# Putting out half of the channels during the last pass of attention: a two-layer convolution and attention kernel on one core

## The chip, the core and the metric

The kernel runs on one core of a Trainium2 chip. The metric is device time in microseconds, from the start of the program on that core to its end. Times below that carry a position, such as "at 3327.8", are counted from the start of the profiled span.

## What is computed

Two layers work on `x`, 2 images of 512 channels and 64 x 64 pixels in float32. The first is a deformable convolution with a residual; the change doesn't touch it. The second is attention within each image, a product with `Wfc`, a batch norm and a ReLU, and again a residual. Cut to its core:

```python
q = tanh(px @ Wq.T); k = tanh(px @ Wk.T); v = px @ Wv.T
attn = softmax(einsum('bip,bjp,p->bij', q, k, align_w))
content = (px + attn @ v) @ Wfc.T + bfc
c = transpose(content, (0, 2, 1))                  # images, 512 channels, pixels
mean, var = over images and pixels, per channel
x = x + relu(gamma * (c - mean) / sqrt(var + eps) + beta)
```

Mean and variance of a channel are over both images and all pixels. So no value of a channel can be put out before the last pixel of the last image has its content in that channel. Channels don't depend on each other.

## The kernel before

**Layout.** The 512 channels lie as 4 blocks of 128 partitions. The kernel calls blocks 0 and 1 the lower half (h = 0) and blocks 2 and 3 the upper half (h = 1). The 4096 pixels of an image are 8 columns of 512 (`qb`). A piece is one half by one column, [128, 2, 512] in float32, 0.524 MB; the result is 2 images x 8 columns x 2 halves = 32 pieces. The second layer's input, the residual of the last step, lies in DRAM as `x1_d`; the content before the norm goes to DRAM as `c_d`.

**Attention.** Images are taken in order, n = 0 and 1. In each, four chunks of two columns of queries are worked through; a chunk is 63 slots (7 products over 9 groups of keys), and a slot keeps TensorE busy for about 3 us (`slot`, with `products` at line 1501). After every ninth slot `collect` (1524) takes the sum out of PSUM; it is a generator that is resumed slot by slot. In the 54th slot the last product that the lower half needs ends; `finish` (1509) scales by the softmax's totals, adds the bias, and takes batch norm statistics into `bst` (1522) for that half, by slot 57. The product that ends with slot 62, the last, completes the upper half. The content of the last chunk (image 1, columns 6 and 7) isn't written to DRAM but stays on chip, in `kept`.

**Tiles.** A ring of 38 tiles of a piece's size (`piece`, 1252) feeds the whole stage: keys' exponentials, contents, residuals. In the last chunk of the last image it is less and less used. From slot 22 on, one call of `fetch` (1264) per slot lends free tiles to the final stage: it loads the residual `xr` (1267) and, where it isn't kept, the content `cr` (1271) of the next piece in the list `waiting`. The rule for it is `live + len(taken) + 2 <= 36`, where `live` counts the tiles that attention still needs. Three further tiles, two of the keys' and one of the queries', are lent first (`spare`). These loads are issued by POOL (`nc.gpsimd`), and each waits there until its ring tile is free. SP (`nc.sync`) issues the attention's own loads of `v` (1487) in the meantime, three slots ahead. Behind the last slot come `at.rest()`, which finishes the last `collect`, loads by SP for the rest of the ring (up to 34 taken), and for 8 fresh tiles (`fin`, 1810).

**The final stage.** One batch norm of all four blocks (1815 to 1822) gives scale and shift. Then for each piece, in the order image 1 before image 0, column by column, both halves of a column in turn: two ReLU activations with scale and shift on ACT (1829), one add of the residual on DVE (1832), one store on POOL (1833). The tile of the residual is then free for the next load, the tile that is stored after three further pieces; refills are issued by SP. The program ends with a test whether the fast path was allowed (551 to 570): a small identity matrix (`ident_f`) made on POOL, a transpose on TensorE, three steps on DVE, a register load on every engine, and a branch around the general path, whose code is long.

Engines issue their own instructions in program order and wait on semaphores. In this stage the order is written by hand (`manual_schedule`), so the order of calls in the source is the order in each engine's queue, except for the closing test, which stands outside of it.

Of the kernel before, what the change touches and what calls it, by code (L numbers as in the profile page):

```python
# [10 lines left out]
F32 = mybir.dt.float32  # L11
I32 = mybir.dt.int32
AF = mybir.ActivationFunctionType
# [5 lines left out]
P = 128  # L19
NB = 2  # L20
# [554 lines left out]
def window_path(ctx: ExitStack, tc: tile.TileContext, t_in: dict, out: bass.AP, far: bass.AP, sums: bass.AP):  # L575
# [67 lines left out]
    with ExitStack() as l0:  # L643
# [298 lines left out]
        def fetch(i, s):  # L942

            if i >= NSEQ:
                return
            n, ch = divmod(i, NCH)
            t = io.tile([P, PX, C], F32, name="patch", bufs=2)
            for p in range(PX):
                nc.sync.dma_start(
                    t[:SN, p, :], xt_d[n][ch * ROWS + PR * s : ch * ROWS + PR * s + SY, PC * p : PC * p + SX, :]  # L950
                )
            patches[i, s] = t
# [289 lines left out]
    with ExitStack() as l1, tc.manual_schedule():  # L1242
# [15 lines left out]
            taken.append(name)  # L1258
            return piece(name)

        waiting = deque((n, qb, h) for n in reversed(range(NB)) for qb in range(NCH) for h in range(2))
        ready = deque()

        def fetch(new, queue):
            n, qb, h = waiting.popleft()
# [8 lines left out]
        with ExitStack() as inner:  # L1274
# [33 lines left out]
            def sum_pixels(engine, pair):  # L1308

                (a_lo, a_hi), (b_lo, b_hi) = pair  # L1310
                s = [piece("xs") for _ in range(4)]
                engine.tensor_add(s[0], b_lo, b_hi)
                engine.tensor_sub(s[1], s[0], a_lo)
                engine.tensor_sub(s[2], a_lo, b_lo)
                engine.tensor_sub(s[3], a_hi, s[1])
                return s
# [53 lines left out]
            def query_tile():  # L1370
                return lent.tile([P, 2, CH], F32, tag="q", name="q")
# [348 lines left out]
            for n in range(NB):  # L1720
                at = Attention(n)
                first = at.chunks[0]

                for i in range(NCH // 2):
                    if 0 < i < 3 or n and i == 0:
                        k = i + 1 if i else 1
                        pixels[k] = load_pixels(n, k, nc.gpsimd)
                    pk = pair_bank("pk")
                    for h in range(2):
                        for kb in range(KB):  # L1730
                            nc.tensor.matmul(
                                pk[:, h, :], wkq[:, kb, h : h + 2].rearrange("p h d -> p (h d)"),
                                pixels[i][h][kb // 2][:, kb % 2, :], start=(kb == 0), stop=(kb == KB - 1),
                            )
                    qt = piece("qt", (P, CH))
                    for h in range(2):
                        rk, rq = slice(h * DQ, (h + 1) * DQ), slice((1 - h) * DQ, (2 - h) * DQ)
                        nc.scalar.activation(qt[rq], pk[rq, h, :], AF.Tanh)
                        nc.scalar.activation(keys[rk, i, :], pk[rk, h, :], AF.Tanh)
                    nc.scalar.activation(qt, qt, AF.Identity, scale=al)  # L1740
                    for h in range(2):
                        nc.scalar.dma_start(q_d[n][i][:, h, :], qt[(1 - h) * DQ : (2 - h) * DQ, :])
                    if i == 0:
                        first.q = load_queries(n, 0)
                    if i:
                        psums[i] = sum_pixels(nc.vector, pixels[i])
                    for t in range(4):
                        if t % 2 == 0:
                            raw = []
                        raw.append(piece("vform", (P, 2, 4, P)))  # L1750

                        def between(stage):
                            event = EARLY.get((i, t))
                            if event and stage == 2:
                                for done in at.open:
                                    settle(*done)
                                produce(first, *event)
                                at.open = [(first, *event)]
                            step(2)

                        values(t, pixels[i], psums[i], wc, wcs, raw[-1], between)
                        if t in (1, 2) and i + 1 < NCH // 2:
                            for h in range(2):
                                normalize(pixels[i + 1][t - 1][h], 2 * h, *norms[n])
                        if t % 2:
                            g = 2 * i + t // 2
                            fill.append(filling(*raw, v_d[n][g], piece if g + 1 == NG else None))
                        if i == 3 and t == 2:
                            for s in range(3):
                                at.fetch(s)  # L1770
                    pixels.pop(i)
                    psums.pop(i)
                for s in range(LEAD):
                    at.sums(s)
                for s in range(NCH // 2 * SLOTS):
                    if s == 0:
                        at.at(-7, first, s)
                    if s == 2:
                        at.at(-3, first, s)
                    at.slot(s)  # L1780
                    if s < 5:
                        step(2)
                    if n == 0 and s in (92, 94, 96, 98, 101, 103):
                        next(later, None)
                    l = s - (NCH // 2 - 1) * SLOTS
                    if n + 1 < NB:
                        if l == 47:
                            pixels[0] = load_pixels(n + 1, 0, nc.gpsimd)
                        if l == 49:
                            wc = value_output()  # L1790
                        if l == 51:
                            wcs = sum_value_output(wc)
                        if l in (52, 53):
                            for h in range(2):
                                normalize(pixels[0][l - 52][h], 2 * h, *norms[n + 1])
                        if l == 55:
                            psums[0] = sum_pixels(nc.vector, pixels[0])
                    elif l >= 22:
                        if l == 22:
                            room = key_tile()  # L1800
                            spare = deque((room[:, 0:2], room[:, 2:4], query_tile()))
                        live = 6 + sum(last + g >= l for last in (18, 41, 45, 54) for g in range(NG + 1))
                        if len(spare) > 1 or live + len(taken) + 2 <= 36:
                            fetch(lambda name: spare.popleft() if spare else ring_piece(name), nc.gpsimd)
                at.rest()
                if n + 1 == NB:
                    while len(taken) + 2 <= 34:
                        fetch(ring_piece, nc.sync)

        fin = l1.enter_context(tc.tile_pool(name="w1fin", bufs=8, reuse_waits="tile"))  # L1810
        for _ in range(4):
            fetch(lambda name: fin.tile([P, 2, CH], F32, tag="f", name=name), nc.sync)
        bmv = bnp.tile([P, KB, 2], F32, name="bmv")
        for kb in range(KB):
            nc.vector.bn_aggr(bmv[:, kb, :], bst[:, kb, :, :].rearrange("p a b -> p (a b)"))
        bsc = bnp.tile([P, KB], F32, name="bsc")
        nc.scalar.activation(bsc, bmv[:, :, 1], AF.Sqrt, bias=eps)
        nc.vector.reciprocal(bsc, bsc)
        nc.vector.tensor_mul(bsc, bsc, gamma)
        bsh = bnp.tile([P, KB], F32, name="bsh")  # L1820
        nc.vector.tensor_mul(bsh, bmv[:, :, 0], bsc)
        nc.vector.tensor_sub(bsh, beta, bsh)
        free, stored = deque(), deque()
        while ready:
            n, qb, h, ct, xr = ready.popleft()
            ct = kept.pop((qb, h)) if ct is None else ct
            for r in range(2):
                k = 2 * h + r
                nc.scalar.activation(
                    ct[:, r, :], ct[:, r, :], AF.Relu, bias=bsh[:, k : k + 1], scale=bsc[:, k : k + 1]  # L1830
                )
            nc.vector.tensor_add(ct, ct, xr)
            nc.gpsimd.dma_start(out_v[n, :, 2 * h : 2 * h + 2, qb * CH : (qb + 1) * CH], ct)  # L1833
            free.append(xr)
            stored.append(ct)
            if len(stored) > 3:
                free.append(stored.popleft())
            while waiting and len(free) > 1:
                fetch(lambda name: free.popleft(), nc.sync)


# [45 lines left out]
```

## Time and profile before

| what | value |
|---|---|
| median of 3 runs | 3409.13 us |
| lowest, highest | 3407.39, 3413.03 us |
| the profiled execution's own time | 3413.08 us |
| its span | 3411.3 us |
| PE busy | 3152.2 us (92%) |
| DVE busy | 2755.0 us (81%) |
| ACT busy | 1349.5 us (40%) |
| POOL busy | 435.7 us (13%) |
| last product of attention ends at | 3327.8 us |
| first store of a result is issued at | 3340.58 us |
| last store is issued at | 3398.05 us |

The profile is of one execution. Its page gives busy time by engine, the span in 40 equal slices, the DMA queues, the chain of work that ended last, and the costliest groups of instructions. Its trace can be asked for any stretch of the span: which instruction ran when, what it waited for, and how many bytes DMA moved. PE is TensorE, DVE VectorE, ACT ScalarE, POOL GpSimd; SP only issues DMAs. A name such as `out<-cr` means that `out` is written from tiles that the program calls `cr`. A tile keeps the name of its first use: a refill can be `cr<-wx`, a residual loaded into a tile once named `cr`; `wx` is `x1_d` and `wc` is `c_d`.

### The profile page before, as it was taken

The numbers are of one execution on the slowest core, as the hardware profiler recorded it, in microseconds if no ns is written. First come the engines' busy times: TensorE is split into PE (matmuls) and PEld (weight loads), VectorE is DVE, ScalarE is ACT, GpSimd is POOL, SyncE is SP. The second block draws the span as 40 slices with busy tenths as digits, with TensorE's granted clock in tenths as the row PEclk, the third lists the DMA queues.
The fourth block names the chain that finished last, engine by engine and source line by source line (L and its number), as shares of the span: only waits on it lengthen the run. The fifth ranks groups of instructions, "written<-read, shape, count | busy, mean of one in ns | idle before, by whom it ended". The sixth has DMA issues, their size and how long they took to land. (4 is left out here: it accounts for less than half of the span.)

```text
span 3411.3 us, 38291 instructions
## 1 busy us (share of the span) xinstructions
PE 3152.2 (92%) x14147; PEld 2265.2 (66%) x14147; DVE 2755.0 (81%) x3826; ACT 1349.5 (40%) x1802; POOL 435.7 (13%) x474
## 2 busy tenths in 40 slices
PE   5789999999999899899999999999899999999990
PEld 2355555555555567687787877887587787787880
DVE  8899999998999568786885976968697696885975
ACT  2477788788877533202213112023211202203105
POOL 2112111211121001001001010000101101001112
PEclk9799999999999999999999999999999999999995
DMA  6333443344333268758658667657866758658788
GB/s 227 104 99 116 136 125 111 93 127 128 101 97 117 98 233 268 235 181 236 190 167 222 197 192 207 202 189 247 256 196 193 208 185 236 185 170 223 240 296 356
DMA packets 238388, 629.98 MB, mean 185 GB/s; under 512 B 28112, under 2 KB 45136, under 8 KB 237168
## 3 DMA queue, kind: packets, MB, share of 16 engines
q1 hardware_dynamic: 181456, 431.07, 37.8%
q0 software_dynamic: 43936, 159.40, 18.0%
q10 hardware_dynamic: 12800, 36.97, 3.0%
q8 instruction: 114, 1.87, 0.2%
q14 instruction: 82, 0.67, 0.1%
HBM read 410.15 MB, written 124.91 MB: 157 GB/s over the span
## 5 line engine op out<-in xcount | busy, mean ns | idle before, releaser
L1501 PE MATMUL accy<-tt,v 128*128 128x256 f32 x2016 | 601.3, 380 | 0.8 <-DVE ct L1530 0.6
L1413 ACT ACTIVATE e<-pS 128x1024 f32<-128x1024 f32 x256 | 248.3, 1021 | 727.2 <-PE pS L1408 723.0
L1501 PE MATMUL accx<-e,v 128*128 128x256 f32 x1792 | 471.6, 386 | 0.0
L1501 PE MATMUL accy<-e,v 128*128 128x256 f32 x1792 | 461.3, 380 | 0.0
L820 DVE SCALAR_TENSOR_TENSOR conv<-xn,L_conv_dw_w_sb,conv 128x504 f32<-128x504 f32 (+1 forms) x512 | 409.4, 808 | 37.5 <-ACT conv L814 23.6
L1501 PEld LDWEIGHTS accy<-tt,v 128*128 128x128 f32 x2016 | 384.3, 191 | 53.8 <-DVE ct L1530 1.0
L1501 PEld LDWEIGHTS accx<-e,v 128*128 128x128 f32 x1792 | 334.2, 191 | 120.8 <-issue 80.6
L1501 PEld LDWEIGHTS accy<-e,v 128*128 128x128 f32 x1792 | 342.2, 191 | 46.1
L1480 DVE TENSOR_TENSOR tt<-e 128x256 f32<-128x256 f32 x448 | 187.7, 419 | 178.5 <-PE accy L1501 149.6
L1481 DVE TENSOR_TENSOR tt<-tt,e 128x512 f32<-128x512 f32 x448 | 310.0, 692 | 15.3
L1501 PE MATMUL accx<-tt,v 128*128 128x256 f32 x1008 | 301.3, 381 | 5.1 <-DVE tt L1480 5.1
L984 PEld LDWEIGHTS pa<-bt,patch 96*128 96x128 f32 x2048 | 249.6, 196 | 57.5 <-issue 34.9
L1408 PE MATMUL pS<-q,keys 64*128 64x512 f32 x1024 | 257.9, 623 | 15.3 <-ACT e L1413 15.3
L984 PE MATMUL pa<-bt,patch 96*128 96x128 f32 x2048 | 253.5, 281 | 7.7 <-ACT bt L970 6.3
L970 ACT COPY bt<-pb 96x1024 f32<-96x1024 f32 x124 | 235.1, 2009 | 58.1 <-PE pb L965 58.1
L789 PE MATMUL pq<-in_w,xn 128*128 128x512 f32 x512 | 240.5, 614 | 6.8 <-DVE o L882 4.6
L1004 PE MATMUL py<-dT,L_conv_out_w_sb 128*128 128x512 f32 x512 | 236.6, 607 | 4.8 <-ACT dT L995 4.8
L1506 ACT COPY u<-accx 128x256 f32<-128x256 f32 x56 | 20.8, 372 | 519.7 <-PE accx L1501 517.0
L1501 PEld LDWEIGHTS accx<-tt,v 128*128 128x128 f32 x1008 | 192.2, 191 | 32.0 <-DVE tt L1480 6.3
L877 PE MATMUL po<-om_w_pg,feat 128*128 128x432 f32 x512 | 204.8, 546 | 2.3 <-ACT feat L860 2.3
L995 ACT COPY dT<-pa 32x256 f32<-32x256 f32 x496 | 179.6, 362 | 66.0 <-PE pa L984 56.7
L1422 POOL DMA_DIRECT2D tot<-e x144 | 124.0, 887 | 583.5 <-DVE e L1398 277.7
(242 smaller groups left out, 4331.4 us busy)
## 6 DMA issues: line engine op xcount, KB each, us to landing
v<-wv SPq DMA_DIRECT2D x436, 448.0 KB
tot<-e POOLq DMA_DIRECT2D x176, 512.0 KB, 7.0
patch<-xt SPq DMA_DIRECT2D x256, 192.0 KB
v<-ww SPq DMA_DIRECT2D x56, 448.0 KB
wv<-vform SPq DMA_DIRECT2D x48, 512.0 KB
wv<-vsum SPq DMA_DIRECT2D x48, 384.0 KB
xt<-xj SPq DMA_DIRECT2D x128, 128.0 KB
res<-in_x SPq DMA_DIRECT2D x64, 256.0 KB
```

The lines of the kernel that those rows point to most:

```text
L789: nc.tensor.matmul(pq, xn[:, kb, 1 + 2 * t : 3 + 2 * t, :].rearrange("p r c -> p (r c)"), in_w[:, kb, :], start=(kb == 0), stop=(kb == KB ...
L820: nc.vector.scalar_tensor_tensor(dst, src, wt, dst, ALU.mult, ALU.add)
L877: nc.tensor.matmul(po[:, : 3 * GP], f[:, kb, t * P : (t + 1) * P], om_w[:, kb].rearrange("p a k g -> p (a k g)"), start=(kb == 0), stop=(k ...
L970: copy(bt[:SN].rearrange("s g q d -> s d (g q)")[:, d0 : d0 + 4, :], pb[:SN])
L984: nc.tensor.matmul(pa[:, p], xp[:SN, p, cb * P : (cb + 1) * P], bt[:SN, 4 * cb : 4 * cb + 4, PX * s + p, :], start=True, stop=True,)
L995: copy(dst, src)
L1004: nc.tensor.matmul(py, out_w[:, kb, cb * P : (cb + 1) * P], dT[:, kb, :], start=(kb == 0), stop=(kb == KB - 1))
L1408: nc.tensor.matmul(p[:, a, :], keys[r, i, (2 * u + h) * P : (2 * u + h + 1) * P], c.q[r, qh, :], start=True, stop=True,)
L1413: nc.scalar.activation(e.rearrange("p a q -> p (a q)"), p.rearrange("p a q -> p (a q)"), AF.Exp)
L1480: nc.vector.tensor_sub(t[:, 0], x[:, 1], x[:, 3])
L1481: nc.vector.tensor_add(t[:, 1:3], t[:, 0].unsqueeze(1).to_broadcast([P, 2, HQ]), x[:, 0:3:2])
L1501: nc.tensor.matmul(out, v[:, blk, :], op, start=(first and g == 0), stop=(final and g == NG))
```

## The change

The list of pieces is put in another order: all lower halves (image 1, then image 0), then all upper halves. The batch norm is split in two, of two blocks each (`batch_norm(h)`). The lower one runs behind slot 57 of the last chunk. In slots 58 to 62 one piece each is put out (`put_out`: two ReLUs, an add, a store), and from slot 60 free tiles are refilled at once (`refill`). In turn nothing is fetched ahead in slots 57 to 62. One more tile is lent ahead: `early`, which held the weights of keys and queries and isn't used any longer. Behind the last slot the rest of the ring is filled (SP), then the last `collect` is resumed step by step with a piece put out between the steps, then comes a refill, and the upper norm, with a further piece between its halves. The loop over the remaining pieces is as before.

```diff
-        waiting = deque((n, qb, h) for n in reversed(range(NB)) for qb in range(NCH) for h in range(2))
-        ready = deque()
+        waiting = deque((n, qb, h) for h in range(2) for n in reversed(range(NB)) for qb in range(NCH))
+        ready, free, stored = deque(), deque(), deque()
+        scales = {}
+
+        def batch_norm(h):
+
+            mv = bnp.tile([P, 2, 2], F32, name=f"bmv{h}")
+            for r in range(2):
+                nc.vector.bn_aggr(mv[:, r, :], bst[:, 2 * h + r, :, :].rearrange("p a b -> p (a b)"))
+            sc, sh = bnp.tile([P, 2], F32, name=f"bsc{h}"), bnp.tile([P, 2], F32, name=f"bsh{h}")
+            nc.scalar.activation(sc, mv[:, :, 1], AF.Sqrt, bias=eps)
+            yield
+            nc.vector.reciprocal(sc, sc)
+            nc.vector.tensor_mul(sc, sc, gamma[:, 2 * h : 2 * h + 2])
+            nc.vector.tensor_mul(sh, mv[:, :, 0], sc)
+            nc.vector.tensor_sub(sh, beta[:, 2 * h : 2 * h + 2], sh)
+            scales[h] = sc, sh
+
+        def put_out():
+            n, qb, h, ct, xr = ready.popleft()
+            ct = kept.pop((qb, h)) if ct is None else ct
+            sc, sh = scales[h]
+            for r in range(2):
+                nc.scalar.activation(
+                    ct[:, r, :], ct[:, r, :], AF.Relu, bias=sh[:, r : r + 1], scale=sc[:, r : r + 1]
+                )
+            nc.vector.tensor_add(ct, ct, xr)
+            nc.gpsimd.dma_start(out_v[n, :, 2 * h : 2 * h + 2, qb * CH : (qb + 1) * CH], ct)
+            free.append(xr)
+            stored.append(ct)
+            if len(stored) > 3:
+                free.append(stored.popleft())
+
+        def refill():
+            while waiting and len(free) > 1:
+                fetch(lambda name: free.popleft(), nc.sync)
...
+                    elif l > 57:
+                        put_out()
+                        if l > 59:
+                            refill()
+                    elif l == 57:
+                        for _ in batch_norm(0):
+                            pass
                     elif l >= 22:
                         if l == 22:
                             room = key_tile()
-                            spare = deque((room[:, 0:2], room[:, 2:4], query_tile()))
+                            spare = deque((room[:, 0:2], room[:, 2:4], query_tile(), early))
                         live = 6 + sum(last + g >= l for last in (18, 41, 45, 54) for g in range(NG + 1))
                         if len(spare) > 1 or live + len(taken) + 2 <= 36:
                             fetch(lambda name: spare.popleft() if spare else ring_piece(name), nc.gpsimd)
-                at.rest()
                 if n + 1 == NB:
                     while len(taken) + 2 <= 34:
                         fetch(ring_piece, nc.sync)
+                    for _ in at.ends.pop():
+                        put_out()
+                    refill()
+                    norm = batch_norm(1)
+                    next(norm)
+                    put_out()
+                    next(norm, None)
+                at.rest()
...
-        for kb in range(KB):
-            nc.vector.bn_aggr(bmv[:, kb, :], bst[:, kb, :, :].rearrange("p a b -> p (a b)"))
...
         while ready:
...
+            put_out()
+            refill()
```

## What was predicted before the run

> **What bounds the kernel now.** I read the busy shares first, then the table of stretches at the end of the run, then the chain of waits, then single instructions. Over the whole span TensorE is busy 92%, but the change touches only the last 120 us, so that stretch is read alone. Columns: stretch, length, busy time of PE, its weight loads, DVE, ACT, POOL with counts, granted clock, DMA share, GB/s.
>
> ```profile
> 3292.00:3304.00 12.00, 12.00 (x57) 10.60 (x56) 6.81 (x12) 0.37 (x1) 2.11 (x4) 1.00 1.02 410
> 3304.00:3316.00 12.00, 12.00 (x58) 10.58 (x57) 10.83 (x16) 2.56 (x4) 1.58 (x3) 1.00 0.98 351
> 3316.00:3320.00 4.00, 4.00 (x20) 3.54 (x19) 0.00 (x0) 0.00 (x0) 0.00 (x0) 1.00 0.62 230
> 3320.00:3328.00 8.00, 7.76 (x36) 6.49 (x35) 0.89 (x2) 0.37 (x1) 0.00 (x0) 1.00 0.48 171
> 3328.00:3336.00 8.00, 0.18 (x2) 0.11 (x2) 7.08 (x11) 2.62 (x3) 0.00 (x0) 0.66 0.48 159
> 3336.00:3344.00 8.00, 0.37 (x1) 0.08 (x1) 6.06 (x17) 6.79 (x11) 2.58 (x5) 0.50 0.98 349
> 3344.00:3404.00 60.00, 0.00 (x0) 0.00 (x0) 34.82 (x29) 38.96 (x55) 21.15 (x30) 0.50 1.03 418
> 3404.00:3408.00 4.00, 0.00 (x0) 0.00 (x0) 0.00 (x0) 0.00 (x0) 0.00 (x0) 0.50 0.52 212
> ```
>
> Three things: TensorE sets the pace until 3327.8; DMA moves 418 GB/s, its ceiling here, from 3344 to 3406; and between them is a hole, 3316 to 3344, where DMA is half idle. The hole is worth (188·4 + 247·8 + 259·8 + 69·8)/418 = 12.8 us of full DMA. But DMA is also full, or nearly, from 3292 to 3316, with loads ahead for the final stage. The chain of waits over the last 107 us agrees that DMA is the tail:
>
> ```profile
> 3352.10 17.19 DMA out<-cr
> ...
> 3369.84 18.84 DMA out<-cr
> ```
>
> Loads (hardware queue, SP) and stores (software queue, POOL) share it about evenly while both have work (3352 to 3388; packets, MB, share):
>
> ```profile
> q0 software_dynamic: 2156, 7.84, 53.3%
> q1 hardware_dynamic: 1997, 7.25, 49.2%
> ```
>
> The program's very end, from the instructions of line 570, the closing test's branch and what follows it (engine, operation, duration in ns, first and last start):
>
> ```profile
> L570 POOLq EVENT_SEMAPHORE  x5: 17/43/43, 3405.2 to 3406.7; - x5
> L570 PEldq COMPARE_BRANCH  x1: 6455/6455/6455, 3339.2 to 3339.2; - x1
> ...
> L570 POOLq COMPARE_BRANCH  x1: 45/45/45, 3399.2 to 3399.2; - x1
> L570 POOLq INC_SWDGE_SEM  x1: 622/622/622, 3408.0 to 3408.0; - x1
> ```
>
> Each engine jumps over the untaken general path. POOL's jump lasts 3399.2 to 3405.2, 6.0 us (PE's 6.5), hidden: the last store, issued at 3398.05, lands at 3408.0. From there to the end of the span are 3.3 us.
>
> **What the Trainium skill says.** "DMA: Bandwidth & Descriptors", queues, rings and completion order: each DMA engine takes turns between queues with work, a packet at a time. The 7.84 against 7.25 MB agree. The same page, where 436 GB/s comes from: the fabric's ceiling is 435 GB/s; the trace holds 418, so no schedule can make the tail's bytes cheaper. "Runtime: NRT & Kernel Launch", instruction fetch mechanics: a branch to a page not in the window waits for a DMA that fetches it. The jumps of 6.0 and 6.5 us agree, and both were taken beside full DMA.
>
> **The change, part by part.** A tile is 0.524 MB, 1.25 us at 418 GB/s. The final stage has 60 tile loads (32 residuals, 28 contents, four being kept on chip) and 32 stores; the change alters none of these counts, so only idle DMA can be won or lost.
>
> *Loads ahead given up.* Before, one fetch per slot is allowed from slot 22 to 62: POOL issues 32 tile loads, the last seven at 3294.4 to 3312.5, and SP four more at 3318.3 to 3327.4. After, fetches stop at slot 56, because 57 is the norm and 58 to 62 put out. Counting with the kernel's own rule for live tiles, they are 14 fetches, 26 tiles: 4 lent plus 22 of the ring. Ring tiles come free when products end, and the 22nd did so at 3291.4. So POOL loads nothing from there until its first store. Seven tiles, 3.67 MB, leave the 10.05 MB that moved from 3292 to 3320; one lent tile moves ahead of 3292. This is a loss of about 7·1.25 - 1.25 = 7.5 us of DMA work not done ahead.
>
> *First half put out early.* The statistics of slot 57 end at 3313.9. Two aggregates (0.54 each, half of the four at 3334.2) end at 3315.0; from aggregate to first Relu took 1.40 (3336.10 to 3337.50), so 3316.4. The 1.28 us table load lies on an idle ACT. Two Relus 1.52, one add 1.23, 0.31 to the issue: first store 3319.5, the next three 1.41 apart, to 3323.7. The fifth stands behind the last copy of `accx` on ACT (3326.12 + 0.37), so 3329.5. TensorE pays nothing: ACT and DVE are idle from 3316 to 3326, DVE's sums for slot 62 slip by some 2.5 us to 3317.5 and are due at 3324.7, and the last attention load is issued at 3315.7, ahead of any store. If that cover failed, it could cost these 2.5 us. The copy on ACT stands behind puts 1 to 4, but their loads were issued by 3220, so they wait for nothing.
>
> *SP's queue.* Six refills stand ahead of the eleven ring loads. Four follow the first four adds (3319.3 to 3323.5), the fifth waits for the first store to land, the sixth for the fifth add (3329.3); only then come the ring's eleven, free or not. The first nine transfers give 11.3 us of work from 3320.5, to about 3331.8, so the queue stays fed.
>
> *Between the last products.* Three puts are woven into the last collect: 3 adds of 1.23 and 2 Relus of 0.8 delay the upper norm by about 6 us, its Relus are first needed by the 17th put, and DMA has the eleven loads meanwhile. Cost nothing; 6 us if DMA were empty there.
>
> *Sum.* From 3320.5 on, 34 loads and 32 stores remain: 66·0.524 = 34.6 MB, 82.8 us. The first 8 us of such a start ran at 349 (3336 to 3344): +1.3. So 3404.6 with no gap. Now loads (34) do not finish well ahead of stores as before (last load at 3388.3), but last, so the last put is load, Relus, add, issue in a row: 1.52 + 1.23 + 0.31 and about 1.5 until data flow, against some two stores still queued (2.5): a gap of 2.0. DMA ends at 3406.6, the last store lands at 3408.6: +0.6 against 3408.0. Bounds: -3 (no ramp, no gap) to +4 (loads get the smaller share).
>
> *The closing test.* In the built program its two POOL instructions on `ident_f` moved from ahead of the 32 stores to behind them, and TensorE, DVE and all branches wait for them. The last store is issued some 4.2 us ahead of landing (the least shown for `cr`), 3404.4. Then POOL's issue 0.73, the two instructions 0.57, transpose 0.45, three DVE steps 0.67, register load 0.5 to 1.1 (0.9 taken): 3407.7. Then the jump. Beside full DMA it was 6.0; here DMA is all but empty, which no row of before shows. Lower end 1 us, upper 6.5; I take 3.5, since its 16 KB (six packets, 0.05 MB for three engines in the last 24 us) wait for nothing. 3411.2 against landing 3408.6; plus 3.3: the span ends at 3414.5 against 3411.3, +3.2. The profiled execution took 3413.08, 3.95 above the median 3409.13; I carry the difference over to the median: 3412.3.
>
> **The rivals.** *Hole filled for nothing (faster).* If what is lost from 3292 to 3320 were not work done ahead, the hole's 12.8 minus ramp 1.3, gap 2.0 and test 2.6 leaves -6.9; with the test hidden, -9.5: 3400. For it: the hole is plain. Against it: DMA at 351 to 410 GB/s ahead of it is loads of the final stage. *The test's jump in full (slower).* The test stands behind the last store and its jump takes 6.5 as on PE, while loads, with 48% of the shared DMA, end about a microsecond later: 3.2 + 3.0 + 1 = +7.2, 3416.3. It decides from a jump of 0.9 us on (3408.6 - 3407.7), where the landing no longer hides it; for it, the jumps that the trace shows take over 5 us. *Not what it says*: the built order shows the puts ahead of the last products, so no more than a remainder.
>
> **Chances.** A measurement of this kernel tells 0.2%, 6.8 us, from no change. Forecast (3412.3, within 0.2%): 0.64. Filled hole, 3400: 0.12, nearly all of it faster by over 0.2%. Full jump, 3416: 0.24, its centre at the bound, its upper part and some of the forecast's tail slower by over 0.2%. So faster 0.11, same 0.66, slower 0.23. Range 3403 to 3418: the lower end lies between forecast and filled hole, the upper takes in the bounds +4 of DMA and the full jump, short of both at their worst.
>
> **What would show it.** DMA near 150 GB/s between 3300 and 3319, then full from 3321 without a hole to about 3404: right. First store near 3319.5, fifth near 3329.5. Last load landing within 8 us of the last store's issue. The test's register loads after the last store, on all engines together, and POOL's jump ending after the last landing. I am wrong if DMA stays full from 3300 to 3319, if it has a new hole near 3325 to 3345, or if TensorE ends later than 3327.8.

## The result and the profile after

| | before | after |
|---|---|---|
| median, 22 runs each | 3407.17 us | 3412.29 us |
| lowest, highest | 3401.20, 3413.03 us | 3408.44, 3416.08 us |
| ratio, 95% interval | | 1.0015 [1.0009, 1.0021] |
| span of the profiled execution | 3411.3 us | 3409.4 us |
| last product of attention ends at | 3327.75 us | 3320.16 us |
| from there to the end of the span | 83.55 us | 89.24 us |

The change costs 5.1 us, 0.15%: less than the 0.2% bound that the prediction set for "no change", and resolved from zero. Forecast were 3.2 us. The interval of the ratio is 3.1 to 7.2 us, so the forecast lies at its lower end.

The two profiled spans can't be subtracted. The execution of after reached the end of the products 7.6 us earlier, for reasons ahead of the change (a load of `xq` that POOL issues some 240 us ahead of the products' end starts at 3078.5 there and at 3086.1 in before, already 7.6 apart), so I compare **tails**: the time from the end of the last product to the end of the span, 83.55 against 89.24 us, +5.7. One tail of one execution is good to perhaps 2 us. In five profiles whose final stage has the same code (after and, below, e1, e5, e10 and e11; e5 only adds small steps to it) the last store is issued 78.7, 76.4, 77.2, 76.3 and 75.6 us behind the products' end: after's is the latest.

The stretches of after, with the same columns as in the prediction. The same place in before lies 7.6 us later.

```profile
3292.00:3304.00 12.00, 12.00 (x57) 10.58 (x56) 11.03 (x17) 2.19 (x4) 0.00 (x0) 1.00 0.55 169
3304.00:3316.00 12.00, 12.00 (x57) 10.55 (x57) 9.86 (x16) 7.70 (x11) 2.45 (x4) 1.00 0.61 192
3316.00:3320.00 4.00, 4.00 (x20) 3.32 (x18) 0.00 (x0) 1.47 (x3) 0.47 (x1) 1.00 1.01 402
3320.00:3328.00 8.00, 0.35 (x3) 0.11 (x2) 7.48 (x9) 3.13 (x5) 1.61 (x3) 0.83 1.01 385
3328.00:3336.00 8.00, 0.00 (x0) 0.00 (x0) 4.03 (x6) 3.81 (x7) 1.30 (x2) 0.50 1.02 399
3336.00:3344.00 8.00, 0.00 (x0) 0.00 (x0) 6.82 (x10) 8.00 (x12) 3.07 (x5) 0.50 1.03 419
```

The hole behind the products is gone: 385 to 419 GB/s where before had 159 to 349. In its place DMA runs at 169 and 192 GB/s during the last slots. Counted back from the products' end, in steps of 4 us from -28 to -8, before moved 400, 380, 333, 338 and 234 GB/s there, and after 221, 122, 165, 172 and 119. The hole has moved ahead of the products' end. TensorE is busy for the whole of each stretch up to 3320.

The stores that were to begin early, from the instructions of the tile `out` and the timeline (start, duration, engine, line):

```profile
3311.51 0.73 POOL L1288 DMA_DIRECT2D out<-keys  x1 [27.21 <-DVE keys L1287]
3321.87 0.73 POOL L1288 DMA_DIRECT2D out<-cr  x1 [5.39 <-DVE cr L1287]
```

These are the first store, 8.65 us ahead of the products' end, and the fifth, 1.71 behind it. The end of the run, from the timeline:

```profile
3394.84 1.52 ACT L1284 ACTIVATE cr<-cr,bsh,bsc 128x512 f32<-128x512 f32 x2 [3.46 <-DMA cr<-wc]
3396.39 1.23 DVE L1287 TENSOR_TENSOR cr<-cr,xr 128x1024 f32<-128x1024 f32 x1 [3.76 <-ACT cr L1284]
3398.89 0.73 POOL L1288 DMA_DIRECT2D out<-cr  x1 [5.23 <-issue]
3399.62 0.22 POOL masks.py:197 MEMSET ident_f<- 128x128 f32 x1
```

Read the gaps between these rows. The Relus behind the last load start at 3394.84, the add ends at 3397.62, yet the store is issued only at 3398.89: 1.27 us later instead of the 0.3 of the pieces just ahead of it, and the row names nothing that it waited for ("issue"). In the meantime DMA runs dry (GB/s in the last column):

```profile
3388.00:3392.00 4.00, 0.00 (x0) 0.00 (x0) 0.59 (x1) 1.52 (x2) 0.65 (x1) 0.50 1.02 418
3392.00:3396.00 4.00, 0.00 (x0) 0.00 (x0) 0.63 (x1) 1.16 (x2) 0.73 (x1) 0.50 0.97 391
3396.00:3400.00 4.00, 0.00 (x0) 0.00 (x0) 1.23 (x1) 0.36 (x1) 1.03 (x3) 0.50 0.04 17
3400.00:3404.00 4.00, 0.37 (x1) 0.08 (x1) 0.56 (x3) 0.00 (x0) 0.21 (x1) 0.50 0.36 143
```

That last store lands 3.1 us after its issue, at 3402.0. The end of the program comes 7.4 us later. The instructions of the closing test's branch:

```profile
L570 POOLq EVENT_SEMAPHORE  x5: 17/43/43, 3405.9 to 3406.2; - x5
...
L570 POOLq COMPARE_BRANCH  x1: 45/45/45, 3401.9 to 3401.9; - x1
L570 PEldq COMPARE_BRANCH  x1: 3558/3558/3558, 3401.9 to 3401.9; - x1
...
L570 POOLq INC_SWDGE_SEM  x1: 566/566/566, 3406.3 to 3406.3; - x1
```

All engines branch together at 3401.9, behind the register loads. POOL goes on at 3405.9, 4.0 us later and 3.9 us behind the landing; before, POOL's jump was over 2.8 us ahead of the landing. Another 3.5 us end the span (POOL's last steps, called the exit below).

### The profile page after: what moved, and what is told of

Its sections match the earlier page's. It is cut to its first block, busy times and chain, and to the rows that moved or that the text cites. A ratio compares the mean times of both kernels' runs of the same rounds, so it can differ in the third digit from the quotient of the medians.

```text
span 3409.4 us, 38281 instructions
## 1 busy us (share of the span) xinstructions
PE 3147.5 (92%) x14147; PEld 2260.3 (66%) x14147; DVE 2755.4 (81%) x3830; ACT 1350.9 (40%) x1803; POOL 432.7 (13%) x468
## 4 chain that ended last, share of the span: by engine, by line
PE 69%; DVE 19%; DMA 6%; issue 3%; ACT 2%; POOL 1%; SPq 0%; ACTq 0%; POOLq 0%; DVEq 0%
PE accy L1535 21%; PE accx L1535 17%; DVE conv L820 10%; PE pS L1442 6%; PE py L1004 6%; PE pq L789 5%; PE pa L984 5%; PE pvy L1693 3%; PE pvx L1693 2%; PE pk L1765 1%; DVE e L1464 1%; DMA early<-in_x 1%; DMA tot<-e 1%; DMA wv<-vform 1%; DMA wv<-vsum 1%
## 5 line engine op out<-in xcount | busy, mean ns | idle before, releaser
L1535 PEld LDWEIGHTS accx<-e,v 128*128 128x128 f32 x1792 | 333.5, 190 | 121.0 <-issue 80.2
```

What stands on the lines that cost most here:

```text
L1535: nc.tensor.matmul(out, v[:, blk, :], op, start=(first and g == 0), stop=(final and g == NG))
```

## The experiments

Theory: the DMA part of the change nets to about nothing (loads ahead given up, hole filled), and the closing test, now behind the last store, costs what its chain and jump exceed the landing. Rivals: the test is hidden and DMA costs the 5 us; or the loads given up cost their full price.

The experiments were timed in 9 to 21 runs beside 41 to 53 runs of the kernel before (medians 3408.30, 3408.51 and 3408.70 us in the three groups). "Last store" is its issue, counted from the products' end; "steps" are the two longest parts of the exit: the last semaphore step (INC_SWDGE_SEM in the trace) and the longest DRAIN that POOL takes before the program ends, in us.

| run | us | ratio, 95% interval | last store | tail | steps |
|---|---|---|---|---|---|
| before | | | 70.3 | 83.55 | 0.62 + 1.82 |
| after | 3412.29 | 1.0015 [1.0009, 1.0021] | 78.7 | 89.24 | 0.57 + 1.58 |
| e1 | 3408.50 | 1.0003 [0.9995, 1.0011] | 76.4 | 81.01 | |
| e2 | 3407.56 | 0.9998 [0.9989, 1.0006] | 69.7 | 81.00 | |
| e3 | 3405.70 | 0.9996 [0.9987, 1.0004] | 64.9 | 80.81 | 1.33 + 4.76 |
| e4 | 3407.68 | 1.0003 [0.9994, 1.0011] | 74.5 | 84.91 | 0.56 + 1.58 |
| e5 | 3408.74 | 1.0000 [0.9992, 1.0008] | 77.2 | 84.27 | 0.56 + 1.58 |
| e6 | 3403.62 | 0.9987 [0.9981, 0.9994] | 64.0 | 79.98 | 1.33 + 4.76 |
| e7 | 3406.94 | 0.9994 [0.9986, 1.0003] | 63.9 | 82.02 | 1.33 + 4.76 |
| e8 | 3413.47 | 1.0013 [1.0004, 1.0021] | 70.9 | 87.85 | 1.32 + 4.72 |
| e9 | 3407.22 | 0.9993 [0.9986, 1.0000] | 63.6 | 80.70 | 1.32 + 4.73 |
| e10 | 3416.68 | 1.0028 [1.0018, 1.0038] | 76.3 | 90.63 | 1.33 + 4.77 |
| e11 | 3411.73 | 1.0010 [1.0004, 1.0017] | 75.6 | 86.12 | 0.58 + 1.66 |
| e12 | 3413.66 | 1.0012 [1.0003, 1.0020] | 71.5 | 87.83 | 1.31 + 4.69 |

### e1 and e2: both kernels without the closing test

Both leave out lines 551 to 570 of before (and the same lines of after) and the general path behind them; the fast path is whole.

```diff
     window_path(tc, t_in, out, far, sums)
-    with tc.tile_pool(name="flag", bufs=1) as fp, ...
-    ...
-    with tc.If(again > 0):
-    ...
```

> The changed kernel without the closing test and without the general path behind it (that part of the program is left out; the output comes from the fast path alone, as always with these inputs). Theory: behind the last store's issue the changed kernel runs memset, select, transpose, three DVE steps, a register load and a jump in a row, and only then leaves, 3.3 us after the store could have landed (3405.9 against 3398.9 + 3.7). Without them the end follows the landing: about 3.3 us less than the changed kernel, so +1.8 us on the kernel before (ratio 1.0005). Rival, the whole loss is in DMA and the test is hidden as it was before: no gain, +5.1 us (1.0015).

> The kernel before without the closing test and the general path (left out in the same way). There POOL's jump ended at 3405.2 and the last store landed at 3408.0, so theory and rival both expect next to nothing: -1.0 to 0 us (0.9997 to 1.0). If it gains as much as the changed kernel does without its test, the test's place was not what cost there.

Without the test the changed kernel is 0.9 us slower by the medians, 0.05% by the ratios, with intervals that include no difference; the tails are equal, 81.0 and 81.0. From the last store's issue to the span's end after goes from 10.51 to 4.63 us, before from 13.25 to 11.31: the test costs 5.9 us there and 1.9 here, 3.9 more, as much as the jump in after outlasts the landing. In before it isn't quite free even though its jump is hidden, since the landing at 3408.0 is followed by 3.3 us of steps that e2 has only in part. The rival that the test is hidden in after (1.0015) is not seen.

### e3: loads ahead kept going

Fetches go on in slots 57 to 62, beside the norm and the puts. So that POOL, which waits for free tiles, doesn't hold up stores, SP issues the five early ones.

```diff
-        def put_out():
+        def put_out(queue=nc.gpsimd):
...
-                    elif l > 57:
-                        put_out()
-                        if l > 59:
-                            refill()
-                    elif l == 57:
-                        for _ in batch_norm(0):
-                            pass
                     elif l >= 22:
+                        if l == 57:
+                            for _ in batch_norm(0):
+                                pass
+                        if l > 57:
+                            put_out(nc.sync)
+                        if l == 61:
+                            refill()
...
-                    while len(taken) + 2 <= 34:
+                    while len(taken) + 2 <= 33:
```

> The changed kernel with the loads ahead given back: fetches go on by the same rule in slots 57 to 62 on POOL, the five stores of slots 58 to 62 are issued by SP, refills wait for slot 61, and the last ring fill stops one tile earlier. Theory: the DMA work not done ahead from 3292 to 3316 is what the change loses; six tiles more are loaded ahead, 6 x 1.25 = 7.5 us less behind it, of which a hole of up to 3 us near the end of the products may eat some: -7.5 to -4.5 us on the changed kernel, so -2.4 to +0.6 on the one before (ratio 0.9993 to 1.0002). DMA from 3292 to 3312 at over 300 GB/s, counted with this run's own end of the products. Rival, loads ahead are not the loss (they only ran beside attention's loads): +5 us (1.0015).

The stretches of e3, the same columns:

```profile
3292.00:3300.00 8.00, 8.00 (x38) 7.04 (x38) 6.88 (x10) 0.19 (x1) 1.59 (x3) 1.00 1.03 418
3300.00:3308.00 8.00, 8.00 (x38) 7.04 (x38) 7.75 (x13) 3.99 (x6) 0.53 (x1) 1.00 0.98 343
3308.00:3316.00 8.00, 8.00 (x38) 7.03 (x37) 6.58 (x10) 5.89 (x9) 0.00 (x0) 1.00 0.44 118
3316.00:3320.00 4.00, 4.00 (x20) 3.51 (x19) 0.00 (x0) 0.94 (x2) 0.00 (x0) 1.00 1.05 404
3320.00:3328.00 8.00, 0.88 (x6) 0.38 (x4) 6.95 (x9) 3.67 (x6) 0.73 (x1) 0.75 1.03 369
3328.00:3388.00 60.00, 0.37 (x1) 0.08 (x1) 35.31 (x43) 37.41 (x53) 19.41 (x28) 0.50 1.03 419
```

Now both are had: DMA full with loads ahead until 3308 and full again from 3316, with a hole of 118 GB/s between. Its last store lands 72.4 us behind the products' end; in after, at 81.8, and at 79.5 and 79.4 in e1 and e10, whose code is the same up to there. So the DMA work ends 7 to 9 us earlier; six tiles' loads are 7.5 us. Not separated is what the five stores on SP instead of POOL do in it: they were not run without the loads. The time falls by 6.6 us: the program's own end, with test and exit, now stands 8.4 us behind the last landing instead of 7.4. The test is less of it (POOL's jump ends 1.0 us behind the landing instead of 3.9), and the exit, of which the last experiments speak, is more.

### e4: three stores held back for the gap

In the last loop the stores of three pieces that are ready early are issued just ahead of the last piece, to have DMA work while that piece is loaded, normed and added.

```diff
...
+        keep = []
         while ready:
-            put_out()
+            if len(ready) == 1 and not waiting:
+                for to, ct in keep:
+                    nc.gpsimd.dma_start(to, ct)
+            put_out(keep if len(keep) < 3 else None)
             refill()
```

> The changed kernel with the stores of three pieces that are ready early in the final loop held back and issued just ahead of the last piece's. Theory: in the changed kernel DMA stands still for about 4 us between the last load's landing and the last store's data; three stores (3.75 us) fill it, loads end earlier by the same, and the last store is issued some 3.5 to 4 us sooner: +1.1 to +1.6 us on the kernel before (ratio 1.0003 to 1.0005). Rival, bytes alone set the end and the gap is noise: no gain, +5 us (1.0015).

Ratio 1.0003, tail 84.9 against 89.2. In the four microseconds in which the last add runs (the one of DVE's column) and its store waits, DMA now holds its full rate:

```profile
3392.00:3396.00 4.00, 0.00 (x0) 0.00 (x0) 1.23 (x1) 1.50 (x2) 0.95 (x2) 0.50 1.03 419
```

The gap between last load and last store was real. From 12 us ahead of the last store's issue to its last byte, after moves 292 GB/s in 14.7 us, which is 4.4 us short of 418 GB/s; e4 moves 399 in 15.1, 0.7 short. The tail is 4.3 us shorter.

### e5: the test worked out ahead

The changed kernel with the test's steps put right behind the last products, on an identity, a tile and a bank of PSUM that are there already. Behind the last store only register load and branch remain.

```diff
                 at.rest()
+            test(scales[2], ident, bank("pt_f")[0:1, 0, :P], bank("pa_f")[0:1, 0, 0:1])
...
+    window_path(tc, t_in, out, far, sums, test)
...
-        ident = fp.tile([P, P], F32, name="ident_f")
-        make_identity(nc, ident)
```

> The changed kernel with the closing test worked out right behind the last products, on tiles that are there already; behind the last store stay only the register load on every engine and the branch. Theory (the test's chain of 2.3 us from the last store's issue to the branch lies on the end's path): the branch comes 1.8 us earlier, about 0.5 us being the register load that stays, the jump then ends at about the last store's landing; time after the products' end 89.2 - 1.8 = 87.4 us, ratio to the kernel before 1.0010. Rival (the end is set by the last store's landing, and the chain lies beside it): 89.2 us, ratio 1.0015.

The gain is larger than the theory's 1.8 us: 1.0000 instead of 1.0015, and from the last store's issue to the end 7.06 instead of 10.51 us. The branch follows the store's issue by 0.5 us instead of 3.0, and the jump itself took 3.1 us instead of 4.0 (3402.3 to 3405.4):

```profile
L566 POOLq EVENT_SEMAPHORE  x5: 17/43/43, 3405.4 to 3405.7; - x5
L566 POOLq COMPARE_BRANCH  x1: 45/45/45, 3402.3 to 3402.3; - x1
```

The expectation had counted the chain only from the end of the store's issue, and left the jump as it was. The last store lands at 3405.4 too, 3.7 us after its issue: nothing of the test stands behind the landing any longer. The rival, that in after the landing sets the end and the chain lies beside it, falls.

### e6 and e7: loads ahead, test ahead, and stores held back

e6 joins e3 and e5, e7 adds e4. The edits are those shown.

> Loads ahead kept going in slots 57 to 62 as in the third experiment, and the closing test worked out behind the last products. There the branch started at 3389.2, the jump ended at 3394.1, and a drain of POOL of 4.8 us came behind it; DMA ended at 3391.4, the last store was issued at 3385.6. Theory: the branch comes at about 3386.5, beside DMA that is still full, so that the jump takes 5 to 6.5 us and ends at about 3392.5: 1.5 us earlier; if the long drain came from the place of the test, another 3 us. Time after the products' end 76 to 79.5 us against 80.8, ratio to the kernel before 0.9983 to 0.9993. Rival (drain and landing set the end, wherever the test is): 80.8 us, 0.9996.

> The sixth kernel, and in addition the stores of three early pieces of the last loop are kept back and issued just ahead of the last piece, as in the fourth experiment. Theory: with loads ahead the last loads land well before the stores are through, so that there is no gap to fill: within 1 us of the sixth kernel, ratio to the kernel before 0.9983 to 0.9995. Rival (a gap between the last load and the last store is there too): 2 to 4 us below the sixth kernel, ratio 0.9975 to 0.9985.

e6 is the fastest of all, 3403.62 us, 0.9987 [0.9981, 0.9994] of the kernel before. It is a version that beats both, the kernel before by 0.13%; e9 below, which differs from it by one load of 0.2 KB, has 0.9993, so the size of the gain is less sure than its interval says. Its tail gained only 0.8 us on e3. The branch came at 3385.6 instead of 3389.2, but beside full DMA POOL's jump took 5.4 us (to 3391.0) instead of 4.9, and 2.2 us more went by in its semaphores until the last store had landed. The long drain stayed. e7 brings nothing on top: with loads ahead, the loads are through well before the stores (last add 62.5 us, last store 64.0 us behind the products' end in e6, with stores still queued), so there is no gap to fill. The reason was expected, the size was not: instead of within 1 us of e6, e7 is 2.0 us longer by the tail, its last store landing at 74.8 instead of 72.7, and 3.3 by the medians. Why was not followed.

### e8: only the loads given up

The kernel before, with one edit.

```diff
-                    elif l >= 22:
+                    elif 22 <= l <= 56:
```

> The kernel before with one edit: from slot 57 on nothing is fetched ahead, as in the changed kernel; nothing is put out early. Seven tiles, 8.75 us of DMA, aren't loaded by POOL from 3294 to 3313. Their loads are issued by SP behind the last attention load at 3315.7 instead, where DMA has 6.5 us of room up to 3328 (752 and 1976 kB at 418 GB/s missing to full). Theory: DMA work not done ahead is lost unless a hole takes it; 8.75 - 6.5 = +2 us, ratio 1.0006, between 1.0000 and 1.0010. Rival 1 (loads given up cost their full price): +7.5 to 8.75 us, ratio 1.0022 to 1.0026. Rival 2 (these loads ahead bring nothing, other things set the end): 1.0000 and DMA with the hole still there from 3316 to 3328.

1.0013: more than the 2 us expected, less than the full 7.5. The last store is issued 70.85 us behind the products' end, 70.30 in before: only 0.6 us later. SP did load the seven tiles into the hole, as expected; in e12, the same kernel but for one small load, DMA is at 269 and 385 GB/s in the last 10 us of the products and at 414 behind:

```profile
3312.00:3316.00 4.00, 4.00 (x20) 3.54 (x19) 0.00 (x0) 0.00 (x0) 0.00 (x0) 1.00 0.92 269
3316.00:3320.00 4.00, 4.00 (x20) 3.51 (x20) 0.00 (x0) 0.00 (x0) 0.00 (x0) 1.00 1.00 385
3320.00:3328.00 8.00, 2.66 (x14) 1.95 (x12) 5.25 (x7) 1.45 (x3) 0.00 (x0) 0.92 1.03 414
```

Of the 4.3 us by which the tail is longer, 3.6 are POOL's last steps (6.05 against 2.44 us), which leaves 0.7 us for the loads; the last store lands at 80.8 instead of 80.2. So loads ahead and hole are two places for the same work: one given up alone costs nearly nothing, since the other takes it; one given up and the other filled with stores, as the change does, nets to nearly nothing too; only with both (e3, e6) is there a gain.

### e9 to e12: what makes the exit long

In the runs so far POOL's last semaphore step and drain took 2.1 to 2.4 us in some kernels and 6.0 to 6.1 in others. The longest drain stands last in its row (shortest, middle, longest in ns). First before, then after, then e10, then e6:

```profile
L1883 POOLq DRAIN  x3: 46/107/1824, 3408.6 to 3411.0; - x3
```

```profile
L1907 POOLq DRAIN  x3: 46/107/1579, 3406.9 to 3409.1; - x3
```

```profile
L1907 POOLq DRAIN  x3: 44/107/4769, 3408.3 to 3413.7; - x3
```

```profile
L1904 POOLq DRAIN  x3: 46/107/4764, 3394.9 to 3400.3; - x3
```

The long ones of the first runs (e3, e6, e7, e8) had an even number of POOL's DMAs, the short ones an odd one. Four kernels change that number by small loads at the program's or the layer's start, for e9, e10 and e12:

```diff
-    nc.gpsimd.dma_start(al[:, 0:1], t_in["L1_conv_align_w"])
+    nc.sync.dma_start(al[:, 0:1], t_in["L1_conv_align_w"])
```

and for e11 the loads of `gamma` and `beta` from SP to POOL.

> The sixth kernel with one 0.2 KB load of the program's first instructions (align_w) issued by SP instead of POOL, so that POOL issues 307 DMAs instead of 308. Among the profiles with the closing test POOL's last semaphore step and drain took 0.57 to 0.62 and 1.58 to 1.82 us where POOL had issued 307 or 313 DMAs, and 1.32 to 1.33 and 4.72 to 4.76 us where it had issued 306 or 308. Theory (the long exit goes with an even number of POOL's DMAs): 0.57 and 1.6 us again, the span's end 3.9 us earlier, time after the products' end 80.0 - 3.9 = 76.1 us, ratio to the kernel before 0.9976. Rival (the long exit goes with the jump ending while the last stores were still landing, or with loads ahead as such): 80.0 us, 0.9987.

> The changed kernel with the same edit: POOL issues 306 DMAs instead of 307. Theory (parity): the last semaphore step 1.33 and the drain 4.7 us, time after the products' end 85 to 89 + 3.9 = 89 to 93 us, ratio to the kernel before 1.0026. Rival (the number of POOL's DMAs has nothing to do with it): 0.57 and 1.6 us, ratio 1.0015.

> The changed kernel with two more small loads (gamma and beta of the last norm) issued by POOL instead of SP: 309 DMAs of POOL, odd again. Control of the tenth run. Theory (parity): the short exit, 0.57 and 1.6 us, ratio 1.0015. Rival (a count other than 307 or 313 has the long exit): 1.33 and 4.7 us, ratio 1.0026.

> The eighth kernel (the kernel before, nothing fetched ahead from slot 57 on) with align_w loaded by SP: 305 DMAs of POOL instead of 306. There the time after the products' end was 87.85 us, 4.3 more than before, of which 7.0 - 3.3 = 3.7 us were the exit. Theory: the exit is short again and what is left is the price of the loads given up alone, +0.6 us: 84.2 us, ratio 1.0002. Rival (the price is the loads', not the exit's): 87.9 us, ratio 1.0013.

The parity falls: e9 and e12 have odd numbers, 307 and 305, and the long exit (first e9, then e12):

```profile
L1904 POOLq DRAIN  x3: 44/107/4728, 3403.5 to 3408.8; - x3
L1883 POOLq DRAIN  x3: 44/107/4687, 3404.7 to 3410.0; - x3
```

The rivals that tie it to loads ahead or to stores still landing fall too, by e10, which is the changed kernel but for one 0.2 KB load: long exit, 3416.68 us, 1.0028. e12 met its rival's numbers, but not its reason, since the long exit was still in it. e10 against e11 is the cleanest pair: tails 90.63 and 86.12, medians 3416.68 and 3411.73. The exit is worth 4 to 5 us of the time.

What goes with the exit in every profile is the issue stall of 1 us that after shows at its last store. e4 and e5 have it at the last store too, and a drain of 1579 ns. e11 has it one store earlier:

```profile
3393.80 0.71 POOL L1288 DMA_DIRECT2D out<-cr  x1 [5.26 <-issue]
```

and a drain of 1661 ns, 82 more. In before, stores wait 0.5 us for each other, but one 1.5 us:

```profile
3395.27 2.24 POOL L1833 DMA_DIRECT2D out<-xr  x3 [1.52 <-DMA out<-cr]
```

Three stores follow the first of this row, and the drain is 1824 ns: 1579 + 3 · 82 = 1825.

This stall comes more than once. The timelines show it earlier in the final stage too, as a store issued late and the next one right behind it. First before, then after, then e10:

```profile
3351.38 1.45 POOL L1833 DMA_DIRECT2D out<-cr  x2 [1.61 <-issue]
```

```profile
3342.06 1.45 POOL L1288 DMA_DIRECT2D out<-cr  x2 [1.30 <-issue]
```

```profile
3345.17 1.45 POOL L1288 DMA_DIRECT2D out<-cr  x2 [1.30 <-issue]
```

Seven profiles have two such stalls (before, after, e1, e2, e4, e5 and e11), and in each of them the second comes 21 of POOL's DMAs after the first. The seven kernels with the long exit have only the earlier one, 19 of POOL's DMAs (e3, e6, e7, e9), 20 (e8, e12) or 21 (e10) ahead of their last. So the exit is short where a stall fell on one of the last four DMAs, and long where the next one had not yet come when the program ended. With that, a 0.2 KB load can decide: after stalls at its last store, e10, with one POOL DMA fewer, just doesn't. The 82 ns for each DMA since the stall fit only the short ones: 19 DMAs would make 1579 + 19 · 82 = 3137 ns, and 4764 were measured. The Trainium skill ("DMA: Bandwidth & Descriptors", SWDGE vs HWDGE vs iDMA) says that POOL writes the descriptors of its DMAs into rings; a ring in which room has to be made after every 21 stores of this size would look like this. That is a reading: no run here changed the ring, ahead of the final stage stalls couldn't be told apart from waits for tiles, and why the drain is long when the stall has not come stays open.

## Why the prediction was right, and where it was off

The predicted time, 3412.3, is the measured median. Part of that is luck: it was built on a median of three runs, 3409.13, and the 22 runs of before have 3407.17. As a difference, 3.2 us were forecast and 5.1 measured. Step by step, positions counted from the products' end (3327.75 in the prediction):

- **Loads ahead given up.** Right. POOL loads nothing in the last slots: from -28 to -8 us, DMA moves 160 GB/s on average instead of 337. e8 and e12 add what the prediction didn't say: alone this costs 0.7 us, for SP would have used the hole.
- **First half put out early.** Right. First store at -8.65 us, predicted -8.25; fifth at +1.71, predicted +1.75.
- **SP's queue and the puts in the last collect.** Right. No new hole: 385, 399, 419 GB/s from 3320 to 3344. TensorE pays nothing.
- **Sum of the DMA work.** Right within 1 us. The last store was to land at +80.85; it landed at +81.8 (78.7 + 3.1). The other profiles with this code lie at and below the forecast: 80.9, 79.5, 79.4 and 78.7 (e5, e1, e10, e11). Test-free, e1 and e2, the change costs 0.9 us by the medians and 0.0 by the tails, against 0.6.
- **The gap at the end.** Right but for one term. Predicted were 2.0 us of idle DMA. Measured as in e4, DMA falls short by 4.4 us in after, 2.8 in e1 and 3.0 in e5, and by 2.1 and 1.6 in e10 and e11. The first three have the stall of 1 us at the last store, which the prediction did not have; the last two don't. What after has beyond e1 and e5, some 1.5 us, is not explained.
- **The closing test.** This is the term that was off: 2.6 us predicted behind the landing, 3.9 measured, in after's profile, in e10's and e11's (3.8 and 3.9), and as the difference between e1 and e2. The chain was right (3.0 us to the branch, 3.3 predicted). Two sizes were not. The jump took 4.0 instead of 3.5, inside the bounds that I gave (1 to 6.5). And I let the last store land 4.2 us after its issue, the least that `cr` showed in before; with DMA to itself it took 3.1. The Trainium skill has the price for a lone one ("DMA: Bandwidth & Descriptors", Anatomy of one DMA: about 2.0 us and the bytes at 436 GB/s, by which I estimate 3.2 us for this tile), and the 3.1 measured agree. An earlier landing hides less of the jump.
- **The exit.** 3.3 us predicted, 3.5 measured. That it came out was luck: one POOL DMA fewer, e10, and it is 3.9 us longer.

The terms that exceed their size, landing 1.0, test 1.3 and exit 0.2 us, are the 2.5 us between the predicted tail (86.75) and the profiled one (89.24); in the medians it is 1.9. Of these the test's 1.3 come back in e10 and e11; the landing's 1.0 doesn't, and e11, which has the short exit as well, has a tail of 86.12. Of the rivals, "hole filled for nothing" failed for the reason given against it, and e3 shows what it would have taken. "The jump in full" was right in its place and wrong in its size: from 4.0 us, the jump beside DMA that is all but idle, not 6.5, beside full DMA.

What stays open: why the last load lands at different times in executions of the same code (Relus behind it from 74.7 us in after, from 72.3 in e1), and what POOL's stall and long drain are. e6 and e9 have equal tails, 80.0 and 80.7, but medians 3.6 us apart; that lies ahead of the tail and wasn't followed.

## What to carry to other kernels

Before filling a hole in DMA, look at what the filling displaces: here loads ahead and early stores shared the same issue slots, and only keeping both shortened the work. When work at a kernel's end is made to finish later or in another order, read the very last instructions as well: a test or a branch that was hidden behind queued stores costs what of it outlasts the last store's landing (3.9 us here), and it can be worked out earlier (in e5 nothing of it was left behind the landing). Compare stages from a common event, not from the start of the span, when two executions reach that stage at different times.

## What the runs showed of the hardware

- A branch around a long piece of code: 5.4 to 6.7 us per jump beside full DMA (POOL in before and e6, PE in before and e12), 3.1 to 4.0 us beside DMA that is almost idle (POOL in after, e5, e10, e11), and 4.9 us in e3, where DMA ran empty during POOL's jump.
- A register load on five engines at once took 0.47 to 0.54 us in after, where DMA was idle, and 1.03 to 1.09 us in e3, where it was full.
- POOL's issue of 512 KB stores stalled by about 1 us, and where a profile shows two stalls in the final stage (seven do), they are 21 of its DMAs apart.
- The end of the program isn't a constant: POOL's last semaphore step and drain took 2.1 to 2.4 us or 6.0 to 6.1, and which of them can be decided by a 0.2 KB load issued 3.4 ms earlier (after and e10).
